# Haar and convolution network on one core: filters of two layers first, late Haar work spread out, and column transforms of two batches in float32r parts

## The chip, the cores and the metric

The kernel runs on one core of a Trainium2 chip. The metric is the device time of one execution in microseconds, as the median of several runs. The core has a matrix engine (PE; its weight loads are listed as PEld), a vector engine (DVE), a scalar engine (ACT) and a queue engine (SP) that here only issues DMAs; ACT issues DMAs too. Each engine works through its own instructions in order. A matmul result lands in the accumulator memory PSUM, which is held in banks that rotate.

## The reference

The input is 4 images (batches) of 64 channels of 256 x 256 numbers, all in float32. Four layers follow each other. Layers 0, 1 and 3 are long two-dimensional convolutions whose filter is a product of a row filter and a column filter, so the kernel does them as two one-dimensional ones with Toeplitz matrices. Each filter comes from a small network of sines:

```python
def _implicit_filter(z, w1, b1, w2, b2, w3, b3, wo, freq, t, deltas):
    h = jnp.sin(freq * (z @ w1 + b1))
    h = jnp.sin(freq * (h @ w2 + b2))
    h = jnp.sin(freq * (h @ w3 + b3))
    h = h @ wo
    decay = jnp.exp(-t * jnp.abs(deltas))
    return h * decay
# layers 0, 1, 3
k = jnp.einsum('ijk,imk->ijmk', hx, hy)[0]
k_f = jnp.fft.rfft2(k, s=(fft_size, fft_size)) / fft_size
u_f = jnp.fft.rfft2(x.astype(jnp.float32), s=(fft_size, fft_size))
y = jnp.fft.irfft2(u_f * k_f, s=(fft_size, fft_size))[..., :L, :L]
out = y + x * bias[:, None, None]
```

Layer 2 goes into the Haar basis and back, with channel mixing and a shrink between:

```python
f1 = haar2d(x)
for i in range(v.shape[0]):
    f3 = f1 * v[i]
    f4 = jnp.einsum('bchw,oc->bohw', f3, conv_w[i])
    f5 = jnp.sign(f4) * jax.nn.relu(jnp.abs(f4) - tau[i])
    acc = acc + f5
y = haar2d(acc, inverse=True)
return y + x
```

## The kernel before

**Filters.** At the start a block with pools of its own computes all filters: 3 layers x 2 axes x 3 sine steps. One step is a 64-row matmul (L103, L105), seven DVE instructions (L110 to L119: bias and frequency, range reduction in five, a clamp) and a Sin on ACT (L121). The outputs (L126, L129) go to DRAM as `pad` (L132), from which each channel's Toeplitz tile `t` is loaded with overlapping rows (L158). The same block loads the Haar constants, casts them to float32r (L79, L80), and multiplies the scale tables `vts` by `fac` (L134) into the DRAM tensor `scales` (L135). Everything else follows it.

**Ticks.** The rest is a list of events (tick, place, run). All are sorted by tick and place and emitted in that order; a scheduler then sets the order on each engine.

- `convolutions(b, ticks)` takes a batch's 64 channels through layers 0 and 1: for each of the two axes of both layers a contraction of six matmuls (`contract`, L167 and L168), with the copy `a` on ACT (L176) between the axes and `y` on DVE (L189) after. The last stage writes Haar pairs into the ring `sd` of eight channels (L230, L231) and a copy to DRAM (`keep`, L232). For every group of four channels, `levels` does the remaining seven Haar levels along the rows, fourteen dependent DVE instructions (L240, L241). Then comes the column transform `down`, a matmul with the Haar matrix: in plain fp32 from `sd` (L263), or, for the channels in `in_parts`, as two float32r matmuls (L259) of a high and a low part. `split` makes the parts: a cast on ACT (L251) and a subtraction on DVE (L252) into the tile `sp`, of which there is one buffer. ACT copies the result (L267), and SP stores it as `coef`.
- `mixing(b)` takes 64 groups of coefficients through the channel matmul (L308), the scaling (L325 on DVE, L327 on ACT), abs and sign (L333, L334), the shrink (L335, L340) and the sum into the tile `z` (L344), which fills 128 KB of each partition.
- `inverse(b)` takes each channel back: `zc` (L361), two small matmuls and two transposes (L368, L369), the float32r parts `w` (L371, L372), the column matmul (L381), the sum with `keep` (L385, L388, L389), and then layer 3's convolution with L167, L168, L176 and L189 again. Of the first three batches every third channel is put off: it goes to DRAM (`late`, L399) and gets its layer 3 during the last mixing.

**How they overlap.** Batch 1's convolutions run alone. Then for each batch b: `mixing(b)` runs beside the convolutions of the next batch, which are spread over it and end two ticks past it; at the tick `end`, here called the border, `inverse(b)` begins, while the Haar work of the next batch's last two groups (channels 56 to 63) is still to do, in about 12 ticks. All channels of batch 1 and every other channel of batches 2 to 4 are in `in_parts`.

Of the kernel before, what the change touches and what calls it, by code (L numbers as in the profile page):

```python
# [9 lines left out]
F32 = mybir.dt.float32  # L10
F32R = mybir.dt.float32r
AF = mybir.ActivationFunctionType
ALU = mybir.AluOpType
PSUM = bass.MemoryType.PSUM
DRAM = bass.MemoryType.DRAM

B, C, S, EMB, ORD = 4, 64, 256, 33, 64
P = 128
ROW = S + P

GT = 4
BUFS = {"res": 1, "y": 3, "co": 2}

INV_2PI = float(np.float32(1.0 / (2.0 * math.pi)))
MAGIC = float(1.5 * 2.0**23)

C1 = 6.28125
C2 = 2028.0 / 2.0**20
C3 = float(np.float32(2.0 * math.pi - C1 - C2))
# [3 lines left out]
def ap(t, offset, dims):  # L33
    return bass.AP(tensor=t.tensor, offset=t.offset + offset, ap=dims)
# [3 lines left out]
def conv_seq_kernel(ctx, tc, x, fz, fw, bias, decay, haar, haar_row, factors, vt, taut, wmix, out):  # L38
# [14 lines left out]
    nc = tc.nc  # L53
# [2 lines left out]
    dram = ctx.enter_context(tc.tile_pool(name="dram", bufs=1, space=DRAM))  # L56


    hbt = const.tile([P, P], F32, name="hbt")
    hb = const.tile([P, P], F32R, name="hb")  # L60
    hbr = const.tile([P, P], F32R, name="hbr")
    hrow = const.tile([P, 2, P], F32, name="hrow")
    nc.sync.dma_start(hbt, haar[0])
    nc.sync.dma_start(hrow, haar_row)
    hsinv, ident = hrow[:, 0, :], hrow[:, 1, :]
    wb = const.tile([P, 2, P], F32, name="wb")
    nc.vector.memset(wb, 0.0)
    for r in range(2):
        nc.sync.dma_start(wb[r * C : (r + 1) * C, r, :], wmix)
    bsb = const.tile([P, 3, C], F32, name="bsb")  # L70
    nc.sync.dma_start(bsb, ap(bias, 0, [[0, P], [C, 3], [1, C]]))


    scales = dram.tile([S // 4 // GT, P, 2, GT, 16], F32, name="scales")
    pads = [dram.tile([C, 2, ROW], F32, name=f"pad{layer}") for layer in range(3)]
    with tc.tile_pool(name="filt", bufs=2) as fp, tc.tile_pool(name="fps", bufs=4, space=PSUM) as fps:
        signs = fp.tile([P, P], F32, name="signs", bufs=1)
        nc.sync.dma_start(signs, haar[1])
        nc.scalar.copy(hb, signs)  # L79
        nc.scalar.copy(hbr, hbt)  # L80
        vts = fp.tile([P, 2, S // 4, 16], F32, name="vts", bufs=1)
        nc.scalar.dma_start(vts[:, 0], vt)
        nc.scalar.dma_start(vts[:, 1], taut)
        fac = fp.tile([P, 2, S // 4, 16], F32, name="fac", bufs=1)
        nc.scalar.dma_start(fac, factors)
        dsb = fp.tile([C, S], F32, name="dsb", bufs=1)
        nc.sync.dma_start(dsb, decay)
        zs, ws = [], []
        for layer in range(3):
            z = fp.tile([EMB, S + 2 * ORD], F32, name=f"z{layer}", tag="z", bufs=3)  # L90
            nc.sync.dma_start(z, fz[layer])
            w = fp.tile([ORD, 2, 3 * ORD + 4], F32, name=f"w{layer}", tag="w", bufs=3)
            nc.sync.dma_start(w, fw[layer])
            zs.append(z)
            ws.append(w)
        cur = {}
        both = [(layer, axis) for layer in range(3) for axis in range(2)]
        for step in range(3):
            for layer, axis in both:
                z, w = zs[layer], ws[layer]  # L100
                ps = fps.tile([ORD, S], F32, name=f"fp{step}_{layer}_{axis}", tag="fps")
                if step == 0:
                    nc.tensor.matmul(ps, z[:, S + axis * ORD : S + (axis + 1) * ORD], z[:, :S], start=True, stop=True)  # L103
                else:
                    nc.tensor.matmul(  # L105
                        ps, w[:, axis, (step - 1) * ORD : step * ORD], cur[layer, axis], start=True, stop=True
                    )
                par = 3 * ORD
                u = fp.tile([ORD, S], F32, name=f"u{step}_{layer}_{axis}", tag="u", bufs=3)
                nc.vector.tensor_scalar(  # L110
                    u, ps, w[:, axis, par + step : par + step + 1], w[:, axis, par + 3 : par + 4], ALU.add, ALU.mult
                )

                k = fp.tile([ORD, S], F32, name=f"k{step}_{layer}_{axis}", tag="k", bufs=3)
                nc.vector.tensor_scalar(k, u, INV_2PI, MAGIC, ALU.mult, ALU.add)
                nc.vector.tensor_scalar(k, k, -MAGIC, None, ALU.add)
                for c in (C1, C2, C3):
                    nc.vector.scalar_tensor_tensor(u, k, -c, u, ALU.mult, ALU.add)
                nc.vector.tensor_scalar(u, u, PI_IN, -PI_IN, ALU.min, ALU.max)  # L119
                h = fp.tile([ORD, S], F32, name=f"h{step}_{layer}_{axis}", tag="h", bufs=12)  # L120
                nc.scalar.activation(h, u, AF.Sin)  # L121
                cur[layer, axis] = h
        for layer, axis in both:
            w = ws[layer]
            ps = fps.tile([C, S], F32, name=f"fo_{layer}_{axis}", tag="fps")
            nc.tensor.matmul(ps, w[:, axis, 2 * ORD : 3 * ORD], cur[layer, axis], start=True, stop=True)  # L126
            f = fp.tile([C, ROW], F32, name=f"f_{layer}_{axis}", tag="f")
            nc.vector.memset(f[:, S:], 0.0)
            nc.vector.scalar_tensor_tensor(  # L129
                f[:, :S], ps, 1.0 / (2 * S) if axis == 0 else 1.0, dsb, ALU.mult, ALU.mult  # L130
            )
            nc.sync.dma_start(pads[layer][:, axis, :], f)  # L132
        for i in range(2):
            nc.vector.tensor_mul(vts[:, i], vts[:, i], fac[:, i])  # L134
            nc.sync.dma_start(  # L135
                scales[:, :, i].rearrange("n p g j -> p n (g j)"), vts[:, i].rearrange("p (n g) j -> p n (g j)", g=GT)
            )


    zpool = ctx.enter_context(tc.tile_pool(name="zpool", bufs=1))  # L140
    tp = ctx.enter_context(tc.tile_pool(name="toep", bufs=5))
    io = ctx.enter_context(tc.tile_pool(name="io", bufs=2))
# [2 lines left out]
    psx = ctx.enter_context(tc.tile_pool(name="psx", bufs=2, space=PSUM))  # L145


    z = zpool.tile([P, 2, S, C], F32, name="z")

    sd = zpool.tile([P, 8, 2, 2, P], F32, name="sd")  # L150
    keep = [dram.tile([C, P, 2, 2, P], F32, name=f"keep{b}") for b in range(B)]
    coef = [dram.tile([2, C, P, S], F32, name=f"coef{b}") for b in range(B)]
    late = dram.tile([B, C, P, 2, S], F32, name="late")

    def toeplitz(layer, c, name):

# [48 lines left out]
    def at(tick, place, run, unit):  # L205
        events.append((tick, place, len(events), run, unit))
# [5 lines left out]
                if stage is not None:  # L212
                    at(tick + s, -s, stage, unit)

    def convolutions(b, ticks, in_parts=()):

        st = {}

        def load(c):
            xt = io.tile([P, 2, S], F32, name=f"x_{b}_{c}", tag="in", bufs=3)  # L220
# [13 lines left out]
        def levels(steps):  # L234
            def run(n):
                t = sd[:, n % 2 * 4 : n % 2 * 4 + 4]
                for step in steps:
                    v = t[:, :, :, 0, :].rearrange("p c k (w e) -> p (c k) w e", e=2 * step)
                    even, odd = v[:, :, :, 0], v[:, :, :, step]
                    nc.vector.tensor_sub(odd, even, odd)  # L240
                    nc.vector.scalar_tensor_tensor(even, even, 2.0, odd, ALU.mult, ALU.subtract)  # L241

            return run

        parts = {}
# [28 lines left out]
        for n in range(C // 4):  # L274
            end = ticks[4 * n + 3] + 4
            for s, steps in enumerate([(1,), (2, 4), (8, 16, 32, 64)]):
                at(end + 1 + s, 1, levels(steps), n)
            for j in range(4):
                if 4 * n + j in in_parts:
                    at(end + 3 + j, 2, split, 4 * n + j)  # L280
                at(end + 4 + j, 2, down, 4 * n + j)
        return ticks[-1] + 11

    def mixing(b, start, n_act):

# [139 lines left out]
    def spread(begin, end, n=C):  # L425
        return [begin + i * (end - begin - 1) // (n - 1) for i in range(n)]


    put_off = range(2, C, 3)
    groups = S // 4  # L430
    ready = convolutions(0, range(C), in_parts=range(C))
    ahead = C
    start = ready + 3
    for b in range(B):
        mixing(b, start, 12 if b + 1 < B else 6)
        end = start + groups + 3
        if b + 1 < B:
            ready = convolutions(b + 1, spread(ahead, end + 2), in_parts=range(0, C, 2))
        else:
            convolution(  # L440
                [(i, c) for i in range(B - 1) for c in sorted(put_off)], spread(start - 2, end + 2, (B - 1) * len(put_off))
            )
        inverse(b, end, put_off if b + 1 < B else ())

        start = max(end + C, ready + 3)
        ahead = start - 3
# [38 lines left out]
def _decay():  # L485
    t = np.linspace(0.0, 1.0, S)
    deltas = np.linspace(math.log(0.01) / 1.5, math.log(0.01) / 0.3, C)
    return np.exp(-t[None, :] * np.abs(deltas)[:, None]).astype(np.float32)[:, ::-1].copy()


# [68 lines left out]
```

## Time and profile before

| what | us |
|---|---|
| median of three runs | 3047.55 (3045.93 to 3049.37) |
| the profiled execution | 3052.63 |
| its span, first to last instruction | 3050.6 |
| first `mix` of the four batches begins at | 485.6, 1134.9, 1826.4, 2515.6 |
| `inverse` of the four batches begins at | 896.4, 1588.5, 2279.4, 2796.7 |

The span is told as stretches between these times: the opening with the filters, batch 1's convolutions, and then mixing and inverse in turn. An engine's busy time in a stretch says how much room it has there; its idle time matters only where other engines wait for it. Durations of DVE and ACT instructions overlap the next one a little, so the sum of durations is above the busy time. PE's fp32 matmuls are listed as two instructions each. Of the DMA issues, the 768 Toeplitz loads take 3.9 us from issue to landing, the six `pad` stores 2.5.

### The profile page before, as it was taken

Reading aid. Unit: us, or ns where it says so; the run is one execution under the profiler, and the core shown is the slowest. Engines: PE = TensorE matmul, PEld = TensorE weight load, DVE = VectorE, ACT = ScalarE, POOL = GpSimd, SP = SyncE. Lnnn points to the kernel's source line nnn. Section 1 sums busy time; section 2 is a strip of 40 time slices with the busy share of each in tenths; the row PEclk is TensorE's granted clock in tenths of the full one; section 3 lists DMA queues with packets and bytes.
Section 4 is the critical chain, followed back from the end, with each engine's and each line's share of the span. In section 5 each row is a group of like instructions: output and inputs, shape, how many; then the busy total and the mean of one; then the engine's idle time right before and its main releaser. Section 6 shows DMA issues by size and latency. Waiting matters only on the chain. (4 is left out here: it accounts for less than half of the span.)

```text
span 3050.6 us, 51749 instructions
## 1 busy us (share of the span) xinstructions
PE 2971.9 (97%) x16944; PEld 2615.0 (86%) x16944; DVE 2518.7 (83%) x4549; ACT 2117.0 (69%) x4918; POOL 0.2 (0%) x4
## 2 busy tenths in 40 slices
PE   5999999999999999999999999999999999999999
PEld 2999988888888888888887888888887888888998
DVE  5667768999987878898987878899986889998776
ACT  1333336899885658888885658888885668887554
POOL 0000000000000000000000000000000000000000
PEclk9999999999999999999999999999999999999999
DMA  3777787666667776666667776666667777877776
GB/s 109 215 231 228 233 232 212 199 205 204 200 201 223 237 229 194 206 206 204 202 209 227 239 228 197 207 206 206 203 207 213 242 234 234 235 231 216 212 210 188
DMA packets 562239, 649.36 MB, mean 213 GB/s; under 512 B 44369, under 2 KB 447156, under 8 KB 561844
## 3 DMA queue, kind: packets, MB, share of 16 engines
q1 hardware_dynamic: 445972, 493.18, 56.6%
q10 hardware_dynamic: 116000, 152.87, 14.0%
q8 instruction: 137, 2.24, 0.3%
q14 instruction: 130, 1.06, 0.1%
HBM read 426.40 MB, written 219.48 MB: 212 GB/s over the span
## 5 line engine op out<-in xcount | busy, mean ns | idle before, releaser
L167 PE MATMUL py<-t,a 128*128 128x256 f32 x3072 | 924.5, 383 | 16.6 <-ACT a L176 11.1
L176 ACT COPY a<-pa 128x512 f32<-128x512 f32 x768 | 475.5, 621 | 464.5 <-PE pa L168 352.9
L327 ACT ACTIVATE f<-px,vt 128x64 f32<-128x64 f32 x2688 | 585.0, 348 | 103.2 <-DVE f L325 102.7
L168 PEld LDWEIGHTS py<-t,a 128*128 128x128 f32 x3072 | 584.0, 190 | 79.5
L168 PE MATMUL py<-t,a 128*128 128x128 f32 x3072 | 590.5, 274 | 0.0
L167 PEld LDWEIGHTS py<-t,a 128*128 128x128 f32 x3072 | 491.0, 191 | 89.7 <-issue 32.8
L308 PE MATMUL px<-wb,f 128*128 128x256 f32 x2048 | 499.4, 381 | 7.8 <-ACT f L327 6.8
L308 PEld LDWEIGHTS px<-wb,f 128*128 128x128 f32 x2048 | 364.5, 190 | 54.5 <-ACT f L327 17.8
L335 DVE TENSOR_TENSOR mag<-mag,vt 128x1024 f32<-128x1024 f32 x256 | 312.5, 1221 | 52.8 <-ACT mag L333 51.8
L167 PE MATMUL pa<-t,x 128*128 128x256 f32 x1024 | 307.5, 382 | 9.8 <-DMA t<-pad 9.8
L340 DVE SCALAR_TENSOR_TENSOR mag<-mag,f 128x1024 f32<-128x1024 f32 x256 | 312.0, 1219 | 1.1
L167 PE MATMUL pa<-t,y 128*128 128x256 f32 x1024 | 306.6, 381 | 1.3 <-DVE y L189 1.1
L371 ACT CAST w<-pw 128x512 fp32r<-128x512 f32 x256 | 150.2, 587 | 217.8 <-PE pw L369 208.5
L333 ACT ACTIVATE mag<-f 128x1024 f32<-128x1024 f32 x256 | 289.7, 1132 | 14.4 <-DVE z L344 6.8
L334 ACT ACTIVATE f<-f 128x1024 f32<-128x1024 f32 x256 | 278.7, 1088 | 27.0 <-DVE sd L231 15.6
L361 ACT COPY zc<-z 128x512 f32<-128x512 f32 x256 | 282.2, 1103 | 2.0 <-DVE z L344 0.8
L189 DVE SCALAR_TENSOR_TENSOR y<-x,bsb,py 128x512 f32<-128x512 f32 x256 | 190.4, 744 | 69.2 <-PE py L168 62.3
L385 DVE SCALAR_TENSOR_TENSOR t<-r,pu 128x512 f32<-128x512 f32 x256 | 175.5, 686 | 83.9 <-PE pu L381 76.7
L167 PE MATMUL pa<-t,u 128*128 128x256 f32 x772 | 236.2, 388 | 2.1 <-DVE u L389 1.4
L189 DVE SCALAR_TENSOR_TENSOR y<-y,bsb,py 128x512 f32<-128x512 f32 x256 | 190.3, 743 | 53.2 <-PE py L168 51.8
L189 DVE SCALAR_TENSOR_TENSOR y<-u,bsb,py 128x512 f32<-128x512 f32 x193 | 144.0, 746 | 103.9 <-PE py L168 101.4
L168 PEld LDWEIGHTS pa<-t,x 128*128 128x128 f32 x1024 | 195.7, 191 | 26.8
(65 smaller groups left out, 4430.5 us busy)
## 6 DMA issues: line engine op xcount, KB each, us to landing
t<-pad SPq DMA_DIRECT2D x768, 256.0 KB, 3.9
x<-in_x SPq DMA_DIRECT2D x256, 256.0 KB, 3.8
keep<-sd ACTq DMA_DIRECT2D x256, 256.0 KB, 3.1
coef<-co SPq DMA_DIRECT2D x256, 256.0 KB, 3.4
f<-coef SPq DMA_DIRECT2D x256, 256.0 KB, 3.9
r<-keep SPq DMA_DIRECT2D x256, 256.0 KB, 3.1
out_y<-y ACTq DMA_DIRECT2D x256, 256.0 KB, 3.6
late<-u ACTq DMA_DIRECT2D x63, 256.0 KB, 2.6
```

The costliest lines, as they stand in the source:

```text
L167: nc.tensor.matmul(ps[:, m, :], src[:, 0, m * P : (m + 1) * P], t[:, ::-1], start=True, stop=False)
L168: nc.tensor.matmul(ps[:, m, P:], src[:, 1, m * P : (m + 1) * P], t[:, : P - 1 : -1], start=False, stop=True)
L176: nc.scalar.copy(a, ps)
L189: nc.vector.scalar_tensor_tensor(y, s[res], bsb[:, layer, c : c + 1], ps, ALU.mult, ALU.add)
L308: nc.tensor.matmul(ps[:, h, q, :], f[:, q, h * P : (h + 1) * P], wb.rearrange("p r n -> p (r n)"), start=True, stop=True,)
L327: nc.scalar.mul(f4[:, j], px[:, j], scale(g, 0)[:, j : j + 1])
L333: nc.scalar.activation(mag, f4, AF.Abs)
L334: nc.scalar.activation(f4, f4, AF.Sign)
L335: nc.vector.tensor_sub(mag, mag, over(g, 1, 16))
L340: nc.vector.scalar_tensor_tensor(mag, mag, 0.0, st[g]["f4"], ALU.max, ALU.mult)
L361: nc.scalar.copy(a, z[:, :, :, c].rearrange("p h (i k) -> p h k i", k=2))
L385: nc.vector.scalar_tensor_tensor(t, st[c]["r"], 0.5, ps, ALU.mult, ALU.add)
```

## The change

1. **Filters.** `filters(layer, queue)` computes both axes of a layer at once: the weights of the two axes stand in one block-diagonal 128 x 128 matrix, made on the host, so that one matmul and one DVE instruction serve 128 rows. The working tiles are slices of `z` (`part`), which is written for the first time by batch 1's mixing; the extra pools are gone. Layers 0 and 1 (`one`, `two`) are emitted first, interleaved, each followed by matmuls whose result nobody reads (`warm`, 6 and 9). The constants, the filter of layer 3 (`three`) and the scale tables are put into the tick list, one piece per tick from tick 4. In the built order ACT's cast of hbt and the table load for Sin stand before the first Sin, and hbt's load stands on SP behind the loads of the first three x tiles.
2. **Late Haar work.** `convolutions` gets `border`: events of the last two groups that fall at or past it are moved to three times their distance from it, so they take 36 ticks in place of 12.
3. **Parts.** In batches 3 and 4 every channel is in `in_parts`, in place of every other one. Batch 2 keeps every other.

```diff
+    room = z.rearrange("p h r c -> p (h r c)")
+    free = [0]
+
+    def part(n, parts=P):
+        free[0] += n
+        return room[:parts, free[0] - n : free[0]]
...
+    def filters(layer, queue):
+
+        fz_sb, fw_sb = part(S + P, EMB), part(3 * P + 4)
...
+        def load():
+            nc.sync.dma_start(fz_sb, fz[layer])
+            queue.dma_start(fw_sb, fw[layer])
+
+        def begin(n):
+            ps = bank(f"fp{layer}_{n}").rearrange("p m s -> p (m s)")[:, :S]
+            if n == 0:
+                nc.tensor.matmul(ps, fz_sb[:, S:], fz_sb[:, :S], start=True, stop=True)
+            else:
+                nc.tensor.matmul(ps, fw_sb[:, (n - 1) * P : n * P], st["h"], start=True, stop=True)
+            u, k = st["u"], st["k"] = part(S), part(S)
...
+        def finish(n):
+            u, k, h = st["u"], st["k"], part(S)
+            for c in (C1, C2, C3):
+                nc.vector.scalar_tensor_tensor(u, k, -c, u, ALU.mult, ALU.add)
+            nc.vector.tensor_scalar(u, u, PI_IN, -PI_IN, ALU.min, ALU.max)
+            nc.scalar.activation(h, u, AF.Sin)
...
+        def end():
...
+            nc.vector.scalar_tensor_tensor(f[:, :S], ps, dsb[:, S:], dsb[:, :S], ALU.mult, ALU.mult)
+            for axis, queue in enumerate((nc.scalar, nc.sync)):
+                queue.dma_start(pads[layer][:, axis, :], f[axis * C : (axis + 1) * C])
...
+        def warm(n):
+
+            ps = psx.tile([P, 2, S], F32, name=f"warm{layer}", tag="mix")
+            for i in range(n):
+                nc.tensor.matmul(ps[:, i % 2, :], st["f"][:, :P], st["f"][:, :S], start=True, stop=True)
...
-    def convolutions(b, ticks, in_parts=()):
+    def convolutions(b, ticks, in_parts=(), border=None):
...
+        def after(tick, n):
+            return tick if border is None or tick < border or n < C // 4 - 2 else border + 3 * (tick - border)
...
-                at(end + 1 + s, 1, levels(steps), n)
+                at(after(end + 1 + s, n), 1, levels(steps), n)
             for j in range(4):
                 if 4 * n + j in in_parts:
-                    at(end + 3 + j, 2, split, 4 * n + j)
-                at(end + 4 + j, 2, down, 4 * n + j)
-        return ticks[-1] + 11
+                    at(after(end + 3 + j, n), 2, split, 4 * n + j)
+                at(after(end + 4 + j, n), 2, down, 4 * n + j)
+        return after(ticks[-1] + 11, C // 4 - 1)
...
+    one, two, three = filters(0, nc.scalar), filters(1, nc.scalar), filters(2, nc.sync)
+    one[0]()
+    nc.sync.dma_start(dsb, decay)
+    two[0]()
+    nc.sync.dma_start(bsb, ap(bias, 0, [[0, P], [C, 3], [1, C]]))
+    for do in (one[1], one[2], two[1], one[3], one[4], two[2], one[5], one[6], two[3], one[7], *two[4:7]):
+        do()
+    one[8](6)
+    two[7]()
+    two[8](9)
+    for tick, do in enumerate([constants, None, None, *three[:-1], *tables()], 4):
+        if do is not None:
+            at(tick, 3, lambda unit, do=do: do(), 0)
...
-            ready = convolutions(b + 1, spread(ahead, end + 2), in_parts=range(0, C, 2))
+            ready = convolutions(b + 1, spread(ahead, end + 2), in_parts=range(0, C, 2 if b == 0 else 1), border=end)
```

## The prediction

> **What bounds the kernel now.** I read first the page's busy shares, then the opening on the timeline, then tables of each engine's busy time by stretch, then the groups of instructions by shape, and last the timeline where the TensorE clock fell.
>
> ```profile
> PE 2971.9 (97%) x16944; PEld 2615.0 (86%) x16944; DVE 2518.7 (83%) x4549; ACT 2117.0 (69%) x4918; POOL 0.2 (0%) x4
> ```
> A busy PE is only a pointer, since its spans overlap. But in most stretches PE waits for nobody, so PE's own work and the few places where it waits are the time.
>
> The opening, from the timeline (start, length in us, then who):
> ```profile
> 5.28 0.59 SPq L91 DMA_DIRECT2D z<-in_fz  x1
> 8.38 5.38 PE L103 MATMUL fp<-z 33*64 33x256 f32 x12 [8.38 <-DMA z<-in_fz]
> 9.53 0.54 DVE L110 TENSOR_SCALAR u<-fp,w 64x256 f32<-64x256 f32 x1 [8.13 <-PE fp L103]
> 13.12 0.28 DVE L119 TENSOR_SCALAR u<-u 64x256 f32<-64x256 f32 x1
> 13.43 0.42 ACT L121 ACTIVATE h<-u 64x256 f32<-64x256 f32 x1 [3.83 <-DVE u L119]
> 55.06 2.60 SPq L158 DMA_DIRECT2D t<-pad  x5
> 58.94 1.19 PE L167 MATMUL pa<-t,x 128*128 128x256 f32 x2 [9.75 <-DMA t<-pad]
> 67.79 0.88 PE L167 MATMUL pa<-t,y 128*128 128x256 f32 x2
> ```
> The filters keep DVE in line: 18 steps from 9.53 to 47 us, 2.08 us each. The first convolution starts at 58.94, and its fp32 matmuls follow each other at 0.43 us per 256 columns until 68.3, at 0.22 after: half clock for 9.4 us.
>
> Busy time by stretch; columns: stretch, its length, then PE, PEld, DVE, ACT, POOL, granted clock, DMA share, GB/s:
> ```profile
> 486.00:896.00 410.00, 404.12 (x2183) 350.80 (x2182) 379.49 (x659) 370.49 (x1066) 0.00 (x0) 1.00 0.67 201
> 897.00:975.00 78.00, 72.06 (x399) 61.07 (x398) 56.21 (x117) 43.20 (x66) 0.00 (x0) 0.96 0.69 210
> 1135.00:1588.00 453.00, 450.42 (x2461) 394.13 (x2460) 404.97 (x708) 382.20 (x1088) 0.00 (x0) 1.00 0.67 203
> 2280.00:2355.00 75.00, 68.82 (x383) 58.12 (x382) 52.98 (x116) 38.18 (x60) 0.00 (x0) 0.95 0.72 213
> 2516.00:2796.00 280.00, 272.93 (x1465) 240.09 (x1463) 274.05 (x321) 241.93 (x572) 0.00 (x0) 1.00 0.79 232
> ```
> The first, third and fifth are mixing (batches 1, 2 and 4), the second and fourth are borders where an inverse stage begins while the last Haar work runs. In 1135:1588 DVE has 48 us to spare, ACT 71, PE 2.6.
>
> Groups by shape (busy in all, mean ns of one):
> ```profile
> L259 PE MATMUL pz<-sp,hbr 128*128 128x512 f32 x320 | 116.1, 442 | 9.5 <-ACT sp L251 9.5
> L263 PE MATMUL pz<-sd,hbt 128*128 128x512 f32 x192 | 98.2, 593 | 0.0
> L252 DVE TENSOR_TENSOR sp<-sd,sp 128x512 fp32r<-128x512 f32 x160 | 109.8, 686 | 68.2 <-ACT sp L251 68.2
> L251 ACT CAST sp<-sd 128x512 fp32r<-128x512 f32 x160 | 105.7, 661 | 16.4 <-DVE sd L241 15.0
> ```
> Nearly all that PE waits for a split channel (9.5 us) is three events, one at each border. The first, on the timeline:
> ```profile
> 955.80 0.17 DVE L241 SCALAR_TENSOR_TENSOR sd<-sd 128x8 f32<-128x8 f32 x1
> 956.01 0.62 ACT L251 CAST sp<-sd 128x512 fp32r<-128x512 f32 x1 [1.65 <-DVE sd L241]
> 956.68 0.79 PE L259 MATMUL pz<-sp,hbr 128*128 128x512 f32 x1 [2.94 <-ACT sp L251]
> ```
> The last level (L241) ends late among the inverse's DVE work, the split (L251) follows it, and PE stands. Right after, matmuls go at half speed until 962.6; the trace's clock is halved for 6.83 us here and again at the third border (2341.6 to 2348.4).
>
> **A. Filters (−25.4 us).** Both axes of a layer become one 128-row step: 9 steps for 18, and a step costs DVE the same (durations go by columns), so 2.1 us. Only 6 stand before the first convolution. Layer 0's filter, in us from the span's start: its first load is now first in SP's queue, 0.73 + 3.10 (5.28 to 8.38) = 3.8; matmul to DVE 1.15 (8.38 to 9.53): 5.0; two layers interleaved reach the clamp after 3.6 (9.53 to 13.12): 8.6. Then a new wait: ScalarE's cast of hbt and its table load stand before the first Sin, and hbt's load stands in SP's queue behind the third x load, which waits for layer 0's weights (0.72 + 2.6 to 4.0, the rows of w and vts; I take 4.2). 4.2 + 0.58 + 0.45 for two issues + 3.4 landing (0.73 to the cast at 4.27) + 0.3 + 1.28 table = 10.3 for the Sin; behind it stands the whole chain, 1.4 us late. Sin to next DVE step is 0.86 + 1.15 = 2.0: 12.3. A step alone takes 2.3 to its clamp, Sin 0.3 later: 14.9; third step 16.9, interleaved 3.6: 20.5, Sin at 21.1 (the cast of hb waits for signs just before: 0 to 0.8 us, I take 0.3); the output step ends at 23.5. Pad written 2.6 later: 26.1; Toeplitz load 3.85 (55.06 to 58.91): 30.0.
> PE decides instead: layer 1's output matmul stands behind 6 warm matmuls (6 x 0.86 at half clock, 23.7 to 28.8), its DVE step ends at 30.4, then 9 more warm ones. If full rate comes 9.4 us after PE became dense (22.4), the 9 take 1.2 us at half rate and 3.3 at full: 35.1. Then three contractions of 1.31 us (69.28 to 70.59) and one copy wait of 0.68 bring the first pa<-t,y at 39.7, against 67.79: 28.1 saved. The second pad is issued at 30.5, so its Toeplitz tile is there at 37, in time. Bounds: full rate by 27 gives 34.1 and 29.1 saved; warming that does nothing gives 38.3 and as slow a first part as before, 20.6.
> Given back: layer 3's filter moves into batch 1. Its 4 matmuls cost PE 4 x 0.43 = 1.7. Its DVE (3 x 2.1, the output, two products of 1.2), its 3 Sin of 0.42, its loads of vt, taut, factors and the constants, all on SP among Toeplitz and x loads, lie in a stretch (70 to 420 us) where DVE is idle for 113 us, ACT for 222, and DMA runs at 0.76. Without that cover each of 7 handoffs would hold PE, 0 to 1 us; I take 1 in all. So −28.1 + 2.7 = −25.4; ends −20.6 + 8.7 = −12 and −29.1 + 1.7 = −27.
> [...]
>
> **B. Parts for 64 more channels (−11.3 us).** PE per channel: 98.2/96 = 1.02 becomes 116.1/160 = 0.73; 64 x 0.297 = 19.0 less. Added: 64 x 0.686 DVE and 64 x 0.661 ACT, about 28 of each 32 inside the two mixing stretches: DVE 405 + 19 = 424 of some 444 us (95.5%), ACT 382 + 18.5 = 401 (90%). They lie in the idle time above, but queue ahead of what feeds PE: ACT's copies a (L176), whose late end held PE in 486:896. There ACT is at 90%, DVE at 92.6%, PE idle 5.9 of 410 (1.43%), against 2.6 of 453 (0.57%) in 1135:1588. The fifth stretch has DVE at 97.9% and PE idle 7.1 of 280 (2.5%). In both PE waits for ACT; the nearer is 486:896, with ACT's share the same and the same mixing beside convolutions: +0.86% of 445 us, twice = 7.7. B = −19.0 + 7.7 = −11.3. By the other row 17.2 come back: −1.8. Ends −19 and −1.8.
>
> **C. Late Haar work at every third tick (−16.2 us).** No instruction is added. 8 channels at each of three borders have their levels, split and transform spread from 12 ticks to 36. The three waits (2.94, 2.8, 3.7 = 9.4) go, since three inverse ticks, over 10 us, now lie between a split and its transform; with them the two half-clock spells, 2 x 6.83 x 0.5 = 6.8. Their coef stores move later on SP; they are first read at the next mixing, some 28 ticks on, so nothing waits. What hides the moved work is an inverse stage with DVE idle for 30 of 155 us; gone, the waits only move: 0. Other end: all PE idle in the three borders (5.9, 5.6, 6.2) and the clock: −24.6.
>
> **Sum.** −25.4 − 11.3 − 16.2 = −52.9 against the profiled execution's own 3052.63 us (span 3050.6): 2999.7. The runs' median is 3047.55, 5.1 lower; so 2994.7, and I say 2995.
>
> **Rivals.**
> 1. The mixing stretches take the split's ACT and DVE work badly (fifth stretch's row), and B is −1.8: 3047.55 − 25.4 − 1.8 − 16.2 = 3004. For it: DVE at 95.5%. Against: PE waits there for ACT, which has 10% spare.
> 2. Warming fails and the border waits merely move: −12 − 11.3 + 0 = 3024. For it: PE pauses between the warm groups (fo1 at 28.8, warm at 30.6), and the second border waited 2.8 us without losing clock, so the clock doesn't hang on the wait alone. Against: 5 us of dense matmuls before, and the spread order.
> 3. Slower: the single split buffer. A split waits for the previous channel's matmuls, which PE reaches only in order; if each newly split channel holds PE as at a border (3.1 us), 64 x 3.1 − 60.6 (A, C and B's 19.0) = +138, 3185. It decides from 0.95 us per channel. Against: batch 1 splits every channel with ticks of 5.25 us and PE idle of 0.0 in 350 us.
> 4. The filter chain does not shorten, because a load or a shared-buffer dependency holds it to the old end: +2.7 − 11.3 − 16.2, 3023. The built order shows no such wait.
>
> **Chances.** Forecast 0.68, rival 1 0.17, 2 0.06, 3 0.04, 4 0.03, 0.02 for anything else. 0.2% of 3047.55 (6 us) is about what a measurement tells from no change. Rivals 1, 2 and 4 end faster, 3 slower: faster 0.93, same 0.02, slower 0.05. The range takes in rival 1 and the better ends of A, B and C in part, not all at once (2977): 2982 to 3012.
>
> **What would show it.** First pa<-t,x near 35 us and pa<-t,y near 40; split matmuls 448, unsplit 64; PE idle near 6 us in each of the two mixing stretches; no PE wait for sp over 1 us at a border and no half clock there. Wrong if the first convolution starts after 45, if PE's idle in a mixing stretch passes 12 us, or if the borders still show half clock.

## The result, and the profile after

The changed kernel takes 2994.78 us (median of 4 runs, 2993.65 to 2999.86), the kernel before 3047.62 (4 runs, 3045.93 to 3049.37): ratio 0.983, 95% interval 0.9813 to 0.9847. The profiled execution took 2994.63 us, its span is 2992.8. The prediction, 2995 (2982 to 3012), was right in its total; some of its terms were not, and the sections below say which. (A note to the description of the kernel: one contraction is four matmuls, not six; the profile lists them as eight instructions.)

The page's busy shares of the changed kernel:
```profile
PE 2929.2 (98%) x16950; PEld 2610.1 (87%) x16950; DVE 2535.0 (85%) x4544; ACT 2147.1 (72%) x4973; POOL 0.2 (0%) x4
```
PE's busy time fell by 42.7 us, the span by 57.8: by that count most of the gain is time in which PE was listed as busy, and the rest is waits. The opening, from the timeline (start, length, who):
```profile
9.54 0.30 ACT L156 CAST hbr<-hbt 128x128 fp32r<-128x128 f32 x1 [6.61 <-DMA hbt<-in_haar]
9.85 1.28 ACT L125 ACT_TABLE_LOAD   x1
11.15 0.72 ACT L125 ACTIVATE z<-z 128x256 f32<-128x256 f32 x2
...
22.49 1.22 PE L130 MATMUL fo<-z 128*128 128x256 f32 x2 [4.11 <-ACT z L125]
24.36 4.11 PE L142 MATMUL warm<-z 128*128 128x256 f32 x12
28.31 0.59 PE L130 MATMUL fo<-z 128*128 128x256 f32 x2
29.48 4.15 PE L142 MATMUL warm<-z 128*128 128x256 f32 x18 [0.58 <-DVE z L133]
33.47 0.59 PE L189 MATMUL pa<-t,x 128*128 128x256 f32 x2
35.62 0.70 PE L189 MATMUL py<-t,a 128*128 128x256 f32 x2 [0.68 <-ACT a L198]
38.34 0.60 PE L189 MATMUL pa<-t,y 128*128 128x256 f32 x2
```
The wait for hbt and the table load stand before the first Sin, as foretold; the Sin starts at 11.15 (10.3 was the estimate). The warm matmuls bring PE to full clock before the convolution: its first pair takes 0.59, where the kernel before began with 1.19. Busy time by stretch (stretch, length, then PE, PEld, DVE, ACT, POOL, granted clock, DMA share, GB/s): mixing 1, the first border, mixing 2, 3 and 4.
```profile
462.00:873.00 411.00, 405.32 (x2187) 351.35 (x2186) 379.71 (x660) 371.18 (x1066) 0.00 (x0) 1.00 0.67 201
873.00:951.00 78.00, 75.45 (x460) 66.64 (x459) 64.53 (x133) 47.33 (x70) 0.00 (x0) 1.00 0.75 225
1104.00:1553.00 449.00, 439.86 (x2451) 391.11 (x2451) 417.47 (x730) 396.55 (x1112) 0.00 (x0) 1.00 0.68 205
1783.00:2232.00 449.00, 440.33 (x2455) 391.54 (x2454) 417.28 (x729) 396.29 (x1111) 0.00 (x0) 1.00 0.69 205
2458.00:2738.00 280.00, 272.96 (x1465) 240.13 (x1463) 273.94 (x321) 241.75 (x571) 0.00 (x0) 1.00 0.79 231
```
At the border PE now issues 460 matmul instructions in 78 us at a granted clock of 1.00, where it had 399 at 0.96. In the mixing of batch 2 PE is busy 439.9 of 449 us, where it had 450.4 of 453: less work, but more waiting. Groups by shape (busy in all, mean ns | idle before, who ended it):
```profile
L334 PE MATMUL px<-wb,f 128*128 128x256 f32 x2048 | 503.5, 381 | 16.7 <-ACT f L353 16.7
L285 PE MATMUL pz<-sp,hbr 128*128 128x512 f32 x448 | 160.5, 439 | 0.3 <-DVE w L398 0.3
L278 DVE TENSOR_TENSOR sp<-sd,sp 128x512 fp32r<-128x512 f32 x224 | 153.9, 687 | 83.0 <-ACT sp L277 81.3 <-PE py L190 1.4
L277 ACT CAST sp<-sd 128x512 fp32r<-128x512 f32 x224 | 153.4, 685 | 4.8 <-DVE sd L267 4.8
L289 PE MATMUL pz<-sd,hbt 128*128 128x512 f32 x64 | 32.7, 593 | 0.0
```
448 split matmuls and 64 plain ones, and PE waits 0.3 us for them, where it waited 9.5. The first row is the new wait: mixing's matmul stands 16.7 us for ScalarE's scaling (6.8 before, at L327).

Length of each stage in us and, in brackets, PE's idle time in it, read from the timelines. The opening ends at the first pa<-t,y, batch 1 at the first `mix`; mixing and inverse as before. The last row counts half-clock spells between the opening and the end, by their lengths.

| stage | before | after | filters_only | no_spread | half_parts | all_parts | all_parts_11 |
|---|---|---|---|---|---|---|---|
| opening | 67.8 | 38.3 | 38.0 | 38.4 | 39.1 | 37.9 | 38.3 |
| batch 1 | 417.8 (1.3) | 423.1 (3.4) | 423.7 (3.7) | 423.2 | 423.7 | 420.5 (3.7) | 422.3 (4.9) |
| mixing 1 | 410.8 (5.9) | 411.4 (5.7) | 411.5 (6.0) | 411.6 | 412.0 | 412.6 (10.9) | 405.7 (5.6) |
| inverse 1 | 238.5 (6.0) | 230.7 (2.6) | 239.0 (5.7) | 239.9 (5.0) | 230.5 (1.5) | 226.1 (3.1) | 228.6 (4.0) |
| mixing 2 | 453.5 (2.6) | 449.3 (9.1) | 452.7 (3.3) | 448.9 (9.5) | 452.9 (3.5) | 449.2 (7.7) | 443.1 (1.9) |
| inverse 2 | 238.0 (5.8) | 229.8 (1.6) | 239.4 (5.6) | 243.0 (8.4) | 231.1 (1.6) | 230.6 (2.2) | 228.9 (1.1) |
| mixing 3 | 453.0 (2.2) | 449.5 (8.7) | 452.7 (2.1) | 450.2 (8.7) | 452.8 (2.0) | 448.9 (7.9) | 443.1 (1.8) |
| inverse 3 | 236.2 (6.2) | 225.5 (2.2) | 237.2 (5.8) | 232.8 (5.0) | 229.3 (2.8) | 224.1 (1.3) | 224.4 (1.5) |
| mixing 4 | 281.1 (7.5) | 281.3 (7.7) | 281.4 | 281.5 | 281.2 | 284.9 (9.9) | 281.4 (7.8) |
| half clock | 2 x 6.83 | none | 3 x 3.41, 6.83 | 3 x 3.41, 6.83 | 3.41 | 3.41 | none |

From before to after: opening −29.5, batch 1 +5.3, the two mixing stages −4.2 and −3.5, the three inverse stages −7.8, −8.2 and −10.7. That is −57.8 with +0.8 in mixing 1 and 4, the fall of the span.

### The profile page after: what moved, and what is told of

It is laid out like the page before. It is cut to its first block, busy times and chain, and to the rows that moved or that the text cites. A ratio compares the mean times of both kernels' runs of the same rounds, so it can differ in the third digit from the quotient of the medians.

```text
span 2992.8 us, 51867 instructions
## 1 busy us (share of the span) xinstructions
PE 2929.2 (98%) x16950; PEld 2610.1 (87%) x16950; DVE 2535.0 (85%) x4544; ACT 2147.1 (72%) x4973; POOL 0.2 (0%) x4
## 5 line engine op out<-in xcount | busy, mean ns | idle before, releaser
L334 PE MATMUL px<-wb,f 128*128 128x256 f32 x2048 | 503.5, 381 | 16.7 <-ACT f L353 16.7
L334 PEld LDWEIGHTS px<-wb,f 128*128 128x128 f32 x2048 | 362.6, 191 | 62.1 <-ACT f L353 26.7
L211 DVE SCALAR_TENSOR_TENSOR y<-x,bsb,py 128x512 f32<-128x512 f32 x256 | 190.3, 743 | 57.8 <-PE py L190 49.9
L189 PE MATMUL pa<-t,u 128*128 128x256 f32 x772 | 232.8, 383 | 3.2 <-PE pu L407 3.2
L278 DVE TENSOR_TENSOR sp<-sd,sp 128x512 fp32r<-128x512 f32 x224 | 153.9, 687 | 83.0 <-ACT sp L277 81.3
L190 PEld LDWEIGHTS pa<-t,y 128*128 128x128 f32 x1024 | 194.5, 190 | 26.3
```

Source lines behind the costliest of these rows:

```text
L189: nc.tensor.matmul(ps[:, m, :], src[:, 0, m * P : (m + 1) * P], t[:, ::-1], start=True, stop=False)
L190: nc.tensor.matmul(ps[:, m, P:], src[:, 1, m * P : (m + 1) * P], t[:, : P - 1 : -1], start=False, stop=True)
L211: nc.vector.scalar_tensor_tensor(y, s[res], bsb[:, layer, c : c + 1], ps, ALU.mult, ALU.add)
L334: nc.tensor.matmul(ps[:, h, q, :], f[:, q, h * P : (h + 1) * P], wb.rearrange("p r n -> p (r n)"), start=True, stop=True,)
```

## The experiments

### One part alone, and each part taken away

The three parts can be separated by arguments of the code. The kernel before, run again beside the experiments, took 3047.56, 3049.95, 3050.03 and 3049.24 us in their four sessions, so medians of different sessions do not settle differences of 2 or 3 us. `filters_only` has the new filters alone:
```diff
-in_parts=range(0, C, 2 if b == 0 else 1), border=end)
+in_parts=range(0, C, 2))
```


> The new filters alone; the Haar work at its old ticks, every other channel of batches 3 and 4 in parts as before. Theory (three separate gains): the opening gains 29.5 us, batch 1 gives 5.4 back, so 24 us less than before, about 3024; mixing stretches as before (PE idle about 2.6 us in the second and third), and the three borders again show PE waits for the split cast of about 3 us. Rival (the borders gain because everything starts at another phase): the inverse stages are shorter here too and the time is under 3012.

3028.51 us (3026.24 to 3031.31; before 3047.56 in the same session, 3042.88 to 3050.87); ratio 0.9939 (0.9926 to 0.9951). As the theory has it, PE waits for the split at each border (2.94, 2.81 and 3.34 us) and the inverse stages are no shorter; the time is 4.5 above the 3024 expected. `no_spread` has filters and parts, without the spread:
```diff
-2 if b == 0 else 1), border=end)
+2 if b == 0 else 1))
```


> Filters and parts, without the spreading of the late Haar work. Theory: 24 us from the filters and about 10 from the parts, so 3013; the PE waits for the split cast stand at the borders (9 to 12 us in all) and some of the borders may show a half-clock spell. Rival (the parts made the inverse stages short): the inverse stages after the second and third mixing are as short as in the changed kernel and the time is 2995 to 3000. Second rival (eight splits at a border in place of four make the waits longer without the spread): over 3018.

3023.64 us (3019.51 to 3025.2); ratio 0.9917 (0.9904 to 0.9931): 10.6 above the theory's 3013, and past the 3018 of the second rival. `half_parts` has filters and spread, with every other channel of batches 3 and 4 in parts:
```diff
-in_parts=range(0, C, 2 if b == 0 else 1)
+in_parts=range(0, C, 2)
```


> Filters and spreading, with only every other channel of batches 3 and 4 in parts as before. Theory: 24 us from the filters and 16 to 24 from the spreading, so 3000 to 3008; PE idle in the second and third mixing back at about 2.6 us (9 in the changed kernel), these stretches about 4 us longer each. Rival (the parts' PE time is eaten wholly by new waits): 2995, the same as the changed kernel.

3008.17 us (3006.83 to 3009.7); ratio 0.9872 (0.9858 to 0.9885), at the upper end of the theory. PE's idle in the second and third mixing is back at 3.5 and 2.0 us.

From these medians: the filters are worth 19.0 us, the spread on top of them 20.3, the parts on top of both 13.4. But without the spread the same parts give only 4.9 (3028.51 to 3023.64), and with the parts there the spread is worth 28.9. The two belong together. By the stage table, the three inverse stages of `no_spread` sum to 715.7 us, as without the parts (715.6 in `filters_only`); with the spread the parts take 4.9 from them (690.9 in `half_parts`, 686.0 in the changed kernel). The timeline of `no_spread` shows what stands there (start, length, who, idle before):
```profile
932.04 0.17 DVE L267 SCALAR_TENSOR_TENSOR sd<-sd 128x8 f32<-128x8 f32 x1
932.25 0.62 ACT L277 CAST sp<-sd 128x512 fp32r<-128x512 f32 x1 [1.64 <-DVE sd L267]
932.90 0.69 DVE L278 TENSOR_TENSOR sp<-sd,sp 128x512 fp32r<-128x512 f32 x1 [0.68 <-ACT sp L277]
...
932.92 0.80 PE L285 MATMUL pz<-sp,hbr 128*128 128x512 f32 x1 [2.93 <-ACT sp L277]
```
The border's wait is the old one: last level, cast, PE. In the second inverse stage PE also waits 1.11 us at 1614.04 for a subtraction (L278) that stood on DVE behind a Haar level, and that level had waited 2.15 us for the store `keep`; the waits for `y` grow from 2.1 to 2.8. PE's idle there rises from 5.6 to 8.4 us, the stage from 239.4 to 243.0. The third is shorter than in `filters_only` (232.8 against 237.2), with 3.41 us at half clock in place of 10.24. In the changed kernel the same border reads:
```profile
892.64 0.18 DVE L267 SCALAR_TENSOR_TENSOR sd<-sd 128x8 f32<-128x8 f32 x1
892.85 0.62 ACT L277 CAST sp<-sd 128x512 fp32r<-128x512 f32 x1 [2.18 <-DVE sd L267]
893.99 0.68 DVE L278 TENSOR_TENSOR sp<-sd,sp 128x512 fp32r<-128x512 f32 x1
```
The cast still follows the last level at once, but no L285 stands beside it: PE has other work until its transform's turn comes, at 926.39.

Which of the moved events matters? `levels_early` spreads only the splits and transforms, and leaves the levels at every tick:
```diff
-at(after(end + 1 + s, n), 1, levels(steps), n)
+at(end + 1 + s, 1, levels(steps), n)
```


> The changed kernel with only splits and transforms of the late groups spread; their levels at the old ticks. Theory (what held PE was that a transform stands in PE's order one tick after a split that is late): PE idle at each border stays at 1.5 to 3 us, total within 3 us of the changed kernel. Rival (DVE's crowding by fourteen levels among the inverse's work is the stall): PE waits for DVE's t, w and u come back, PE idle 4 us or more per border, half-clock spells possible, total 3 to 12 us longer.

2998.3 us (2996.77 to 3002.09; before 3049.95); ratio 0.9834 (0.982 to 0.9847). The inverse stages are 231.6, 230.7 and 225.7 us with PE idle 3.0, 2.4 and 2.5: at most 0.9 longer each. So the spread of splits and transforms alone brings nearly the whole worth. As the cast of the changed kernel follows its last level at once and PE doesn't stand for it, what helps is the distance between split and transform. Whether the levels' own spread is worth anything isn't settled: the three stages sum to 688.0 us, and five kernels with levels spread (the changed one, `no_warm`, `hbt_first`, `third_first`, `pieces_apart`) lie between 684.3 and 686.0. Another 2.0 us of the difference lie in the opening and batch 1.

### The opening

`no_warm` leaves out the matmuls whose result nobody reads:
```diff
-    one[8](6)
-    two[8](9)
```


> The changed kernel without the 15 warm matmuls (their result was read by nobody). Theory (they buy the clock): the first convolution starts near 31.7 us, when its tiles land, but at half clock; the first matmul of the second axis' layer (pa<-t,y) comes at 40 to 44 instead of 38.3 and the total is 2 to 6 us longer. Rival (they only stand in the way, the clock comes by itself): pa<-t,y at 36.6, total 1.7 us shorter.

2994.4 us (2989.51 to 2997.52); ratio 0.9817 (0.9804 to 0.9831): by its median the same as the changed kernel. Its timeline:
```profile
31.47 1.19 PE L189 MATMUL pa<-t,x 128*128 128x256 f32 x2 [2.38 <-issue]
...
35.05 1.22 PE L189 MATMUL py<-t,a 128*128 128x256 f32 x2 [0.68 <-ACT a L198]
```
The convolution starts 2.0 us earlier at half clock, and reaches full clock only at 39.8, 8.3 us later. The first pa<-t,y comes at 40.07 in place of 38.34: warming is worth 1.7 us there, as the theory has it, but batch 1 (421.8) gives 1.3 of it back and the total shows none of it.

`hbt_first` puts hbt's load and cast before the filters' loads:
```diff
+    nc.sync.dma_start(hbt, haar[0])
+    nc.scalar.copy(hbr, hbt)
     nc.sync.dma_start(dsb, decay)
```


> The load of hbt second in SP's queue and its cast emitted first, so that the first Sin doesn't wait for it. Theory (the cast and table load are on the chain): first Sin near 9.3 us instead of 11.15, pa<-t,y at 36.5 instead of 38.3, total about 1.8 us shorter (2993). Rival (another link, the second filter's load or the warm matmuls, takes its place): pa<-t,y at 38, total the same.

2995.12 us (2993.7 to 2997.62); ratio 0.9823 (0.9809 to 0.9836). The Sin starts at 9.49 and pa<-t,y at 36.5, 1.8 earlier, as the theory has it; batch 1 is 426.2 us, 3.1 longer (1.5 of it PE's idle, 4.9 in place of 3.4), and by the median nothing remains.

`third_first` computes layer 3's filter with the other two, ahead of batch 1:
```diff
+    three[0]()
-one[7], *two[4:7]):
+one[7], *two[4:7], *three[1:7]):
-*three[:-1], *tables()
+*tables()
```


> All three filters before the first convolution; only the scale tables and constants stay in the ticks. Theory: PE's order puts the third filter's steps ahead of the second one's output, so the opening is 4 us longer (pa<-t,y at 42.5), and batch 1 gets back 2.5 to 4 of its 5.4 us (the four matmuls 1.8, their handoffs 1 to 2); total within 2 us of the changed kernel. Rival (the opening hides it between the steps): opening the same, total 3 us shorter.

2994.76 us (2993.87 to 2996.33); ratio 0.9821 (0.9808 to 0.9834). The opening is 6.5 us longer, in part because the clock halved again for 3.41 us after a PE wait of 3.46; batch 1 is 3.9 shorter (419.2), 1.8 of it the filter's four matmuls and 1.6 PE's idle. `pieces_apart` leaves that filter and the tables in batch 1, but at every third tick:
```diff
+at(4, 3, lambda unit: constants(), 0)
+for i, do in enumerate([*three[:-1], *tables()]):
+    at(7 + 3 * i, 3, lambda unit, do=do: do(), 0)
```


> The changed kernel, but the pieces of layer 3's filter and of the scale tables are put at every third tick from tick 7 on, in place of every tick; the constants stay at tick 4. In the changed kernel batch 1's convolutions take 423.1 us, 5.4 more than before, of which 1.8 is the filter's four matmuls. Theory: the rest, 3.6, is handoffs that meet closely and a Toeplitz tile that came 1.26 us late behind the load of the factors, so further apart batch 1 falls to 420 to 421 and the time by 2 to 3 us (2992). Rival: batch 1 takes back part of any gain of the opening, whatever the cause, as it did when the opening was moved by 2 to 6 us: batch 1 stays at 422.5 to 424 and the time within 1.5 us of 2995.

2994.94 us (2994.23 to 2995.8; before 3050.03); ratio 0.9822 (0.9808 to 0.9835). Batch 1 is 424.4 us: the rival holds, and greater distance alone brings nothing. In the changed kernel's timeline of batch 1 the moved filter's matmuls have no wait, and PE's idle is 3.4 us, of which DVE's y ended 2.0 and a late Toeplitz tile 1.26:
```profile
104.24 0.59 PE L130 MATMUL fo<-z 128*128 128x256 f32 x2
...
104.92 0.48 SPq L167 DMA_DIRECT2D z<-in_factors  x1
...
107.52 1.63 SPq L180 DMA_DIRECT2D t<-pad  x2
...
113.39 1.23 DVE L170 TENSOR_TENSOR z<-z 128x1024 f32<-128x1024 f32 x1 [3.85 <-DMA z<-in_factors]
...
115.72 0.67 PE L189 MATMUL pa<-t,x 128*128 128x256 f32 x2 [1.26 <-issue]
```
That tile was behind the load of the factors in SP's queue. The load, 1024 KB, took 8.4 us (104.92 to 113.30); the Toeplitz load issued after it, at 107.52, landed 8.1 us later, where the median is 4.0, and DVE stood 3.85 us for the factors. `pieces_apart` did not remove this, it moved it: with the factors issued at 184.76, DVE waited 3.05 us for them and PE 1.14 us for a tile at 195.51. In `third_first`, which loads the factors at 41.22, DVE waits 1.90 us for them and no tile is late. So the 5.3 us are 1.8 of matmuls, 2.1 of added idle and 1.4 that no row shows. Over these four kernels and the changed one, opening plus batch 1 is 461.5 to 464.0 us, though the opening alone runs from 36.5 to 44.8.

### The mixing stages

`all_parts` puts batch 2's other 32 channels into parts too:
```diff
-in_parts=range(0, C, 2 if b == 0 else 1)
+in_parts=range(C)
```


> The changed kernel with every channel of batch 2 in parts too (32 more). Theory (DVE then binds the first mixing): DVE's 379.7 us of 411 become 399, PE's 405 become 396, so the stretch stays about 411 us with PE idle of 12 to 15 us in it; total 2992 to 2998. Rival (PE still binds): 9.5 us less with 3 given back, 2988 or less. Second rival (queues in order choke): over 3002.

2990.08 us (2987.75 to 2990.57; before 3047.56); ratio 0.9811 (0.9797 to 0.9824). The time is between theory and rival. The first mixing did not get shorter (412.6), as the theory has it: PE's work there fell by some 4 us and its idle rose from 5.7 to 10.9. But the largest share of the idle, 5.7, ended with the scaling on ScalarE (ACT), where the theory has VectorE (DVE). The gain came in batch 1 (−2.6) and in inverse 1 (−4.6); mixing 4, with a half-clock spell, lost 3.6. `scale_11` goes back to the changed kernel's parts and moves one of the twelve scalings from ScalarE to VectorE in mixing 2 and 3:
```diff
-mixing(b, start, 12 if b + 1 < B else 6)
+mixing(b, start, (12, 11, 11, 6)[b])
```


> The changed kernel, but in batches 2 and 3 the mixing gives ScalarE 11 of a group's 16 scalings, in place of 12, and VectorE 5 in place of 4. Per stretch ScalarE has 64 x 0.22 = 14 us less (396.6 to 383), VectorE about 64 x 0.08 = 5 us more (417.5 to 422.5 of 449). In the changed kernel PE stands 9.1 us in the second mixing stretch, 5.1 of it for the scaling on ScalarE, 2.4 for its copies a. Theory (the splits' casts queue in front of the scaling on ScalarE): PE's idle falls to 4 to 6 us in both stretches and the time by 6 to 10 us (2985 to 2989). Rival (VectorE at 93% is what runs late, and ScalarE waits for it): idle stays at 8 to 9 or rises to 12, time 2993 to 3002.

2985.24 us (2982.12 to 2988.17; before 3050.03); ratio 0.9789 (0.9775 to 0.9802). Its two stretches:
```profile
1110.00:1553.00 443.00, 439.87 (x2448) 391.05 (x2447) 419.44 (x731) 385.27 (x1049) 0.00 (x0) 1.00 0.69 208
1783.00:2226.00 443.00, 441.09 (x2456) 392.27 (x2456) 419.38 (x731) 385.87 (x1049) 0.00 (x0) 1.00 0.69 208
```
PE is as busy as in the changed kernel, in 443 us in place of 449; its idle is 3.4 and 1.9, of which the scaling ended 0.1 each. VectorE is busier (94.7%, 93.0% in the changed kernel), and PE waits 1.1 us for it in mixing 2; in mixing 3 no wait for it shows. So what the parts gave back came from ScalarE's queue: without the added casts (`half_parts`) PE's idle was 3.5 and 2.0, with them 9.1 and 8.7, and with one scaling fewer it is 3.4 and 1.9. (Eleven scalings without the added casts were not run.) Inverse 1 is 3.9 us longer than in the changed kernel (234.6), with a half-clock spell of 3.41 after a PE wait of 2.19 for y.

`best` combines `all_parts` with the pieces at every third tick:
```diff
-in_parts=range(0, C, 2 if b == 0 else 1)
+in_parts=range(C)
+    at(7 + 3 * i, 3, lambda unit, do=do: do(), 0)
```


> The changed kernel with all channels of batch 2 in parts too, and the pieces of layer 3's filter and of the scale tables at every third tick. If the two gains add, 2990.1 of the version with all parts less 2 to 3: 2987 to 2988. If the pieces' distance is worth nothing, 2990.

2988.36 us (2987.61 to 2988.96); ratio 0.98 (0.9787 to 0.9813), 1.7 below `all_parts`, between the two expectations and with overlapping intervals: nothing is settled by it. `all_parts_11` combines `all_parts` with eleven scalings in the first three mixings:
```diff
-12 if b + 1 < B else 6
+11 if b + 1 < B else 6
```


> The changed kernel with all channels of batch 2 in parts too, and 11 of 16 scalings on ScalarE in the mixing of batches 1, 2 and 3. If the gains add: 2985.2 (11 scalings in batches 2 and 3) less 4.7 (all parts: 2990.1 against 2994.8) less 4 to 6 in the first mixing, where PE stands 10.9 us, 5.7 of it for the scaling on ScalarE: 2974 to 2977, PE's idle there 5 to 7. Rival: in the first mixing VectorE would have 392 + 5 = 397 of 410 us, 97%, and becomes what runs late: idle stays at 10 or rises to 13, time 2979 to 2984.

2970.99 us (2969.8 to 2971.67; before 3049.24, 3047.05 to 3051.93); ratio 0.9744 (0.9731 to 0.9757), 24 below the changed kernel: the best of all. Its first mixing and two groups:
```profile
462.00:862.00 400.00, 394.84 (x2174) 349.59 (x2173) 388.60 (x671) 368.28 (x1017) 0.00 (x0) 1.00 0.69 205
```
```profile
L353 ACT ACTIVATE f<-px,vt 128x64 f32<-128x64 f32 x2496 | 548.0, 347 | 77.1 <-DVE f L351 76.4
L334 PE MATMUL px<-wb,f 128*128 128x256 f32 x2048 | 502.0, 381 | 6.4 <-ACT f L353 6.0
```
192 fewer scalings on ScalarE than the changed kernel's 2688, and PE's wait for them is 6.0 in place of 16.7. VectorE is at 97.2% there, and PE waits 3.2 us for it in the stage; its idle is 5.6, so the rival falls. The total is 3 us below what the added gains gave: the stage is 405.7 us, and mixing 2 and 3 stay at 443.1.

## Why the prediction was right, and where its terms were not

**Opening: right, by partly wrong steps.** 28.1 were foretold, 29.5 measured. pa<-t,x came at 33.5 (35.1) and pa<-t,y at 38.3 (39.7). The order of events held: Sin behind the cast, PE deciding the start, one copy wait of 0.68. The first Sin came at 11.15 where the text says 10.3 (its terms add to 10.2), and yet the output matmul that makes PE dense came at 22.49, as estimated (22.4): an error in between of the same size made up for it, which is luck. The term that was off is the clock: 9.4 us of dense work were taken from the kernel before, and full rate came 4.5 us after PE became dense (22.49 to 27.0), the better bound of the text. No row of before shows the 27 of that bound; the changed kernel shows 27.0. In `hbt_first` it took 3.7 (20.83 to 24.5), in `no_warm` 8.3 (31.47 to 39.8). The two long times, 9.4 and 8.3, have a PE wait of 0.68 us inside, the two short ones have none; whether that wait makes the difference was not shown. A DVE step costs the same with 128 rows as with 64, as the text has it: its first instruction takes 0.55 us (L113, 128x256), before 0.54 (L110, 64x256).

**Given back in batch 1: 2.7 foretold, 5.3 measured.** The covers named held for the filter's own matmuls, which have no wait. The 1 us taken for handoffs was the mis-sized term: PE waits more for y, and for one tile behind the load of the factors, which the text had among what DMA had room for. A is thus −24.2 in the profiled pair against −25.4, and −19.0 by the medians of `filters_only`, whose profiled execution still has four half-clock spells at its borders. What sets the length of batch 1 beyond these rows was not tried: the experiments moved the opening by −1.8 to +6.5 us and the median by 0.4 at most (3.5 for `levels_early`, where other things changed). Taken against the kernel before in their own sessions, `no_warm`, `hbt_first`, `third_first` and `pieces_apart` are 2 to 4 us better than the changed kernel, with overlapping intervals.

**Parts: the queue named right, the net nearly right by two errors.** In mixing 2 and 3 the sum made −16.6 for the work of 56 channels and +7.7 for waits, −8.9. Measured: −7.7, with PE's idle up by 6.5 in each in place of 3.9, 13.0 in all, and −20.7 of work. ACT was the releaser, as the text says, but the row that it rejected (17.2 in all) was, if anything, nearer to the waits than the one that it took. That both terms were too small by about as much is luck. PE's time without idle fell by 10.7 and 10.0, though 25 more split channels in the stretch, each 0.31 shorter (0.55 in place of 0.86 from its start to the next matmul's), are only 7.8; no row shows the rest. `scale_11` confirms the mechanism: with less in that queue the two stages are 443.2 and 443.3 us, 10.3 and 9.7 shorter than before. The text had priced the split's work as lying in idle time except for copies a; the larger wait is the scaling, 5.1 of 9.1.

**Spread: mis-sized, 16.2 foretold.** The three waits for the split went, the half clock went, and the coef stores on SP cost nothing seen. Between a cast and its transform lie 33.5 us at the first border and as little as 7.8 at the second, where the text had over 10. There each next cast follows as soon as a transform frees the one `sp` buffer (transforms end at 1564.54 and 1570.24, casts start at 1565.13 and 1570.83), and PE doesn't wait for it. The half clock isn't always gone with the spread: `half_parts` and `scale_11` have one spell each, after PE waits of 1.41 and 2.19 us for y at a border. But the inverse stages lost 26.7 in the profiled pair, and 24.7 between `filters_only` and `half_parts`: the far end, 24.6, was the better value. The text counted three waits of 9.4; PE's other idle in the border stages went as well (17 to 5.9 in that pair). The clock made 6.8 of it by the text's estimate, half of two spells of 6.83. The remaining 6.7 are PE spans that are themselves shorter, which no wait shows. The median of the same pair gives 20.3. The parts' rest at the borders was put at −2.4; it interacts with the spread, which no row of before could show.

**Why the total still came out.** The terms sum to −52.9; the profiled pair differs by 58.0, the medians by 52.8. The text carried the 5.1 us by which the profiled execution of before stood above its median over to after; but the profiled execution of after stands at its median (2994.63 and 2994.78). So a sum 5.1 too small met an offset 5.1 too large: that the total is within 1 us is luck. What the sum lacked lies in the inverse stages (−26.7 in place of −16.2 and −2.4); filters, mixing 2 and 3 and the two other mixings together gained 3.2 less than the sum has. The borders may be where that offset lived: before's runs spread over 3042.88 to 3053.62 in all sessions with granted clocks of 0.997 to 0.999, while the changed kernel's have 0.999 to 1.0. That is argued, not shown.

**Rivals.** The first (mixing stretches take the parts badly, 3004) was near in mechanism: 13.0 of gross gain were given back, 7.7 foretold, 17.2 in the rival; its total is off because the gross gain and the spread were larger. The second falls: no half clock, and no border wait for the split; the longest wait left at a border is 1.10 us, for y, at 890.15. The third falls: one `sp` buffer costs PE nothing away from the borders. The fourth falls with the opening.

## What to carry to other kernels

Work that was moved to a queue with 10% to spare was not free here, where it came in pieces of 0.7 us in front of what feeds the bound engine and PE's idle rose by 13.0 us in two stages: read which instruction of that queue the bound engine waits for, and move one small piece of it to the engine beside it. Separate a producer from its consumer in the written order where a stage changes; here that distance was worth 20 us, and 29 once more work was put there. A large load in the queue that feeds the bound engine wasn't free either, with idle time there on average: the load of the factors, 1024 KB in 8.4 us, made the tile behind it 1.26 us late. And when a sum is made against a profiled execution, don't carry its distance to the median over to a kernel whose irregular waits are gone.

## What the runs showed of the hardware

The half-clock spells between the opening and the end last 3.41 or 6.83 us. Five PE waits at the borders, and the clock beside them:

| run | PE waits | until | clock |
|---|---|---|---|
| before | 2.94 us | 956.68 | half from 955.83, for 6.83 us |
| before | 2.81 us | 1650.21 | full |
| before | 3.70 us | 2342.85 | half from 2341.64, for 6.83 us |
| scale_11 | 2.19 us | 893.13 | half from 894.54, for 3.41 us |
| half_parts | 1.41 us | 2267.45 | half from 2267.65, for 3.41 us |

The second border of the kernel before kept its clock through 2.81 us, and in `half_parts` half clock followed a wait of 1.41. So the length of the one wait does not tell whether the clock falls, which bears out the doubt in the prediction's second rival. What does decide it was not shown; no run was made to move a wait.

The price, as an estimate: instructions of 256 columns follow each other at 0.43 us at half clock and at 0.22 at full (before, 60.35 to 61.20 and 68.73 to 69.17 for two), so 6.83 us at half clock cost 3.4 us more than the wait itself, and 3.41 cost 1.7.
